# Causal mask of an attention layer: from matrix products to a select behind the exponential

## The chip, the cores and the metric

The kernel runs on one core of one Trainium2 chip. The metric is the device time of one execution in microseconds. The kernel before was run three times: 1224.71, 1217.82 and 1220.97 us, median 1220.97. One further execution was recorded by the hardware profiler; all rows and timelines here come from it. TensorE does the matrix products, VectorE (DVE) the maxima, ScalarE (ACT) the exponentials and most copies, GpSimd (POOL) some elementwise work and some transfers; SyncE (SP) issues most transfers.

## What is computed

The program is two transformer-like layers on x of shape (2, 1024, 256). Each adds an attention and a feed-forward branch of the normalised x to x. The change is in the attention of layer 0 only, which is causal: 32 query heads of 8 columns share 8 key and value heads.

```python
q = q * cos + rotate_half(q) * sin
k = k * cos + rotate_half(k) * sin
k_rep = jnp.repeat(k, KV_REPEAT, axis=1)
v_rep = jnp.repeat(v, KV_REPEAT, axis=1)
scores = jnp.einsum('bhqd,bhkd->bhqk', q, k_rep) / scale
scores = jnp.where((kpos > qpos)[None, None], -jnp.inf, scores)
attn = jax.nn.softmax(scores, axis=-1)
out = jnp.einsum('bhqk,bhkd->bhqd', attn, v_rep)
```

## The kernel before, in words

Queries are cut into blocks of 128: `(b, i)` is block i of batch b, and the order of the blocks is b = 0, i = 0 to 7, then b = 1, i = 7 to 0. A block attends to key blocks j = 0 to i; j = i is the diagonal, the only one with later keys in it.

**Scores are computed twice.** q and k are split into three bf16 parts each, stacked along the partitions: 64 rows of products (`qst[..][0]`, `kst[..][0]`) and 8 more (`[1]`). Two key heads (e = 0, 1) lie in partitions 0 to 63 and 64 to 127, so that each step issues two matmuls, one for each half of TensorE's rows.

- First, `max_unit` (L832) has queries as rows: it takes one to four heads and up to 512 keys in two PSUM buffers (pool `ps_s`, 3 buffers), and VectorE reduces them to a maximum for each query and head (L855). Only the largest 64 products go into it. On the block of keys with the diagonal the mask is added by matrix products with a half identity `ident_h` (L824): `mask_q`, in bf16, holds -1e30 where the key is later than the query and 0 elsewhere. The contraction runs over 64 rows, so that 128 queries take two products (t = 0, 1) for each half e, four in all. Where the block is 128 keys wide (i = 0 and 4), four heads are masked at once, with the mask broadcast to 512 columns; else each head's last 128 columns are masked in turn.
- Then the maxima are split, turned and written into three further rows of the query tile (`take_max`, `turn_max`), by way of HBM. So the second product gives scores less their maximum.
- `weigh` (L902) has keys as rows: for one key block j and one pair of key heads it makes two PSUM tiles of 128 keys x 512 (four heads x 128 queries; pool `ps_t`, 4 buffers) with products of 64 and of 35 rows (L907). On the diagonal four products with `mask_k` (L824, 512 columns each) add -1e30 for later keys. ScalarE takes the exponential into SBUF tiles `p` (L919, 7 buffers).
- `gather` (L925) multiplies the values, with a column of ones for the sum, by four such tiles (L927), and gathers over j in one PSUM bank, `acc`. After j = i the result is copied, turned, divided by the sum (`normalise`, L939), projected (`output`, L963) and added to x by GpSimd (L970).

**Order.** TensorE's instructions run in the order in which the program is written out (`manual_schedule`); the other engines' are ordered by a scheduler that follows priorities and its own estimate of when an operand is ready. Each engine then works strictly through its own list. The program is written in slots (`one_slot`, L1095). A slot issues as many maxima as a credit allows (the cost of a unit is 2 x heads x width), one piece of the feed-forward branch or of a weight conversion, and whatever an earlier slot put off by `after`; two slots go with each key block, one for each pair of heads. The loop at its end is this:

```python
one_slot(True)
if u and waiting:
    gather(*waiting)
group += weigh(b, i, 2 * G + u, j)
```

So a `gather` stands in TensorE's order two slots and one `weigh` behind the second `weigh` whose tiles it reads. Maxima run some ten slots ahead of their block and are used up about sixteen key blocks' slots before the end.

**GpSimd's other work in this stage:** four operations for each of 16 pieces of the feed-forward output (`out_piece`, L254 to L257), four for each of 12 ternary weight pieces behind VectorE's L332 and L333 (L334 to L337), rotations and splits of later queries and keys (L707, L709, L734), 16 additions to x (L970), a memset of later keys (L745), and transfers that load weights. At the very start it builds `ident_h`, `mask_q` and `mask_k` (L80, L84), ahead of the first weight loads of its queue (L216).

Behind layer 0, from about 800 us on, layer 1 runs; nothing of it is touched.

Of the kernel before, what the change touches and what calls it, by code (L numbers as in the profile page):

```python
# [15 lines left out]
ALU = mybir.AluOpType  # L16
# [3 lines left out]
P = 128  # L20
# [13 lines left out]
HALF = 64  # L34
AUG = 32
EXTRA = AUG + 3
NEG = -1e30
# [11 lines left out]
def two_layers(ctx: ExitStack, tc: tile.TileContext, a: dict, out: bass.AP):  # L49
    nc = tc.nc  # L50
# [22 lines left out]
    both = {}  # L73
    for name, op, fill, sign in (
        ("ident_h", ALU.not_equal, 1.0, 1),
        ("mask_q", ALU.is_ge, NEG, 1),
        ("mask_k", ALU.is_ge, NEG, -1),
    ):
        m = both[name] = zp.tile([P, 2, P], BF, tag=name, name=name)
        nc.gpsimd.memset(m, 0.0)  # L80
        for e in range(2):
            for t in range(2):
                part = m[HALF * e : HALF * e + HALF, t, :]
                nc.gpsimd.affine_select(  # L84
                    out=part,
                    in_=part,
                    compare_op=op,
                    fill=fill,
                    base=sign * HALF * t,
                    pattern=[[-sign, P]],  # L90
                    channel_multiplier=sign,
                )
    ident_h, mask_q, mask_k = both.values()
    groups = cp.tile([P, P], BF, tag="groups", name="groups")
    nc.vector.memset(groups, 0.0)
    nc.vector.memset(groups[0:64, 0:64], 1.0)
# [582 lines left out]
    def attention0(w, qlast, tables):  # L679
# [11 lines left out]
        with ExitStack() as es:  # L691
# [121 lines left out]
                for f in due:  # L813
                    f()

            def add_mask(out, mask, start, stop):

                for t in range(2):
                    for e in range(2):
                        rows = slice(HALF * e, HALF * e + HALF)  # L820
                        rhs = mask[rows, t, :]
                        if len(out[e].shape) == 3:
                            rhs = rhs[:, None, :].to_broadcast([HALF, 4, P])
                        nc.tensor.matmul(  # L824
                            out[e], ident_h[rows, t, :], rhs, start=start and t == 0, stop=stop and t == 1
                        )


# [3 lines left out]
            def max_unit(b, i, pairs, lo, width, part, masked):  # L832
                if (b, i) not in mx:
                    mx[b, i] = pool.tile([P, 2, 2, NH0 // 2], F32, tag="mx", name=f"mx{b}{i}", bufs=3)
                n = len(pairs)
                sc = [ps_s.tile([P, 512], F32, tag="s", name=f"m{b}{i}_{pairs[0]}_{part}{e}") for e in range(2)]
                four = masked and width == P
                if four:
                    add_mask([x.rearrange("p (h k) -> p h k", h=4) for x in sc], mask_q, True, False)
                for s, p in enumerate(pairs):  # L840
                    for e in range(2):
                        rows = slice(HALF * e, HALF * e + HALF)
                        nc.tensor.matmul(  # L843
                            sc[e][:, s * width : (s + 1) * width],
                            qst[b, i][0][rows, p, :],
                            kst[b][0][rows, p // 4, lo : lo + width],
                            start=not four,
                            stop=s == n - 1 if four else not masked,
                        )
                    if masked and not four:  # L850
                        end = (s + 1) * width
                        add_mask([x[:, end - P : end] for x in sc], mask_q, False, True)
                nonlocal reduced
                for e in range(2):
                    reduced = nc.vector.tensor_reduce(  # L855
                        mx[b, i][:, part, e, pairs[0] : pairs[0] + n],
                        sc[e][:, : n * width].rearrange("p (s k) -> p s k", s=n),
                        AX.X,
                        ALU.max,
                        negate=True,  # L860
                    )
# [27 lines left out]
            def max_units(b, i):  # L889

                if i > 3:
                    for p in range(16):
                        yield 1024, lambda p=p: max_unit(b, i, [p], 0, 512, 1, False)
                lo = 512 * (i // 4)
                width = (i % 4 + 1) * P
                n = (4, 2, 1, 1)[i % 4]
                for p in range(0, 16, n):
                    yield 2 * n * width, lambda p=p: max_unit(b, i, list(range(p, p + n)), lo, width, 0, True)
                yield 0, lambda: take_max(b, i)


            def weigh(b, i, u, j):  # L902
                sc = [ps_t.tile([P, 512], F32, tag="t", name=f"s{b}{i}_{2 * u + e}_{j}") for e in range(2)]
                for n, height in enumerate((HALF, EXTRA)):
                    for e in range(2):
                        rows = slice(HALF * e, HALF * e + height)
                        nc.tensor.matmul(  # L907
                            sc[e],
                            kst[b][n][rows, u, j * P : (j + 1) * P],
                            qst[b, i][n][rows, 4 * u : 4 * u + 4, :],  # L910
                            start=n == 0,
                            stop=n == 1 and j < i,
                        )
                if j == i:
                    add_mask([x.rearrange("p (h q) -> p h q", h=4) for x in sc], mask_k, False, True)
                ps = []
                for e in range(2):
                    p = pool.tile([P, 512], F32, tag="p", name=f"p{b}{i}_{2 * u + e}_{j}", bufs=7)
                    nc.scalar.activation(p, sc[e], AF.Exp, scale=scale)  # L919
                    ps.append(p)  # L920
                return ps

# [192 lines left out]
            for n, (b, i) in enumerate(order):  # L1115
                if n and n + 3 < len(order):
                    load_q(*order[n + 3])
                while n not in done_at or slot < done_at[n] + (LEAD if n > 2 else SHORT):
                    one_slot(False)
                for G in range(2):  # L1120
                    for j in range(i + 1):
                        for u in range(2):
# [4 lines that stand above are left out]
                        waiting = (b, i, G, j, group)  # L1127
                        group = []
# [116 lines left out]
```

## Time and profile before

| | |
|---|---|
| median of three runs | 1220.97 us |
| profiled execution | 1217.11 us, its span 1215.3 us |
| busy, of the span | PE 1044.4 us, DVE 738.2, ACT 572.8, POOL 265.4 |
| mean granted TensorE clock | 0.903 |
| 100 to 760 us | PE busy 578.87 us, DVE 540.57, ACT 390.83, POOL 140.39 |
| 760 to 800 us | PE busy 39.53 us, DVE 6.83, ACT 27.90, POOL 7.30 |

In a row of the profile, "L824 PE MATMUL s<-mask_k,ident_h x256" names the line of the kernel, the engine, the operation, the tile that is written and the tiles that are read, and the count. Buffer numbers are left out of names: `s` are the tiles of shifted scores, `m` those of maxima, `p` the exponentials, `acc` the gathered output. Matmuls are pipelined: the start-to-start distance of two rows tells what one costs in a stream, not its own duration. PEld are loads of the stationary operand. A wait "A <- B: total, times, longest" is idle time of A's engine that ended when B was done. The chain that ended last is followed back from the last instruction.

### The profile page before, as it was taken

The numbers are of one execution on the slowest core, as the hardware profiler recorded it, in microseconds if no ns is written. First come the engines' busy times: TensorE is split into PE (matmuls) and PEld (weight loads), VectorE is DVE, ScalarE is ACT, GpSimd is POOL, SyncE is SP. The second block draws the span as 40 slices with busy tenths as digits, with TensorE's granted clock in tenths as the row PEclk, the third lists the DMA queues.
The fourth block names the chain that finished last, engine by engine and source line by source line (L and its number), as shares of the span: only waits on it lengthen the run. The fifth ranks groups of instructions, "written<-read, shape, count | busy, mean of one in ns | idle before, by whom it ended". The sixth has DMA issues, their size and how long they took to land.

```text
span 1215.3 us, 19246 instructions
## 1 busy us (share of the span) xinstructions
PE 1044.4 (86%) x7467; PEld 501.8 (41%) x7484; DVE 738.2 (61%) x1416; ACT 572.8 (47%) x990; POOL 265.4 (22%) x277
## 2 busy tenths in 40 slices
PE   6464897896988989898989998989999999998884
PEld 3233332232332223232323333335676676675673
DVE  7576988886867898788895889253223223323220
ACT  1113353662645757575767775741424414414421
POOL 3021022104053010501014115234313212312100
PEclk9576897997898989997999999999999999999785
DMA  6721001103011010100010110038211421411202
GB/s 193 168 80 37 22 15 38 26 2 90 1 26 27 2 26 18 35 1 18 10 27 3 25 26 5 3 30 120 54 28 45 75 40 45 77 39 28 44 11 53
DMA packets 79012, 49.01 MB, mean 40 GB/s; under 512 B 31720, under 2 KB 73704, under 8 KB 78920
## 3 DMA queue, kind: packets, MB, share of 16 engines
q1 hardware_dynamic: 75960, 43.58, 16.7%
q0 software_dynamic: 2960, 4.20, 1.7%
q8 instruction: 59, 0.97, 0.3%
q14 instruction: 33, 0.27, 0.1%
HBM read 33.59 MB, written 15.73 MB: 41 GB/s over the span
## 4 chain that ended last, share of the span: by engine, by line
PE 57%; DVE 21%; DMA 7%; issue 4%; ACT 4%; POOL 3%; SPq 2%; ACTq 0%; POOLq 0%; DVEq 0%
DVE mx L855 12%; PE acc L927 9%; PE s L907 8%; PE f1gu L610 7%; PE f1o L641 5%; PE m L843 4%; PE sk L520 3%; PE sq L485 3%; PE gu L284 2%; PE m L824 2%; PE s L824 2%; PE ao L586 2%; ACT p L528 2%; DMA qkv<-all 2%; PE acc L535 1%
## 5 line engine op out<-in xcount | busy, mean ns | idle before, releaser
L855 DVE TENSOR_REDUCE mx<-m 128x1 f32<-128x512 f32 (+3 forms) x608 | 373.3, 656 | 114.5 <-PE m L843 66.9
L919 ACT ACTIVATE p<-s 128x512 f32<-128x512 f32 x576 | 307.5, 603 | 163.5 <-PE s L907 115.3
L927 PE MATMUL acc<-p,v 128*9 128x512 f32 x1152 | 165.5, 626 | 0.0
L843 PE MATMUL m<-k,qmain 64*128 64x512 bf16 (+3 forms) x384 | 94.7, 368 | 44.3 <-DVE mx L855 28.4
L610 PE MATMUL f1gu<-xnT,wgu 128*128 128x512 f32 x256 | 118.9, 609 | 0.0
L843 PE MATMUL m<-kmain,qmain 64*128 64x512 bf16 (+3 forms) x384 | 82.4, 335 | 19.9 <-DVE mx L855 18.1
L824 PEld LDWEIGHTS <-ident_h 64*128 64x128 bf16 x1088 | 60.4, 97 | 92.3 <-issue 53.6
L843 PEld LDWEIGHTS <-qmain 64*128 64x128 bf16 x768 | 50.1, 100 | 89.0 <-issue 63.3
L824 PE MATMUL m<-mask_q,ident_h 64*128 64x128 bf16 (+1 forms) x832 | 82.0, 239 | 3.8 <-DVE mx L855 2.8
L618 DVE TENSOR_TENSOR h<-f1gu,h 128x512 f32<-128x512 f32 x32 | 22.1, 692 | 100.4 <-PE f1gu L610 97.0
L907 PE MATMUL s<-qlast,k 35*128 35x512 bf16 x288 | 66.3, 405 | 14.5 <-DMA qlast<-mscr 14.5
L907 PE MATMUL s<-qmain,k 64*128 64x512 bf16 x288 | 68.8, 409 | 11.3 <-ACT ob L252 5.8
L970 POOL TENSOR_TENSOR x<-x,aos 128x256 f32<-128x256 f32 x16 | 12.7, 792 | 300.5 <-ACT aos L969 300.5
L622 POOL TENSOR_TENSOR sq<-h 128x512 f32<-128x512 f32 x28 | 29.1, 1039 | 189.7 <-DVE h L618 189.7
L907 PEld LDWEIGHTS <-k 64*128 64x128 bf16 (+1 forms) x576 | 22.2, 97 | 114.5 <-issue 106.7
L610 PEld LDWEIGHTS f1gu<-xnT,wgu 128*128 128x128 f32 x256 | 48.1, 197 | 49.4 <-issue 49.3
L907 PE MATMUL s<-qmain,kmain 64*128 64x512 bf16 x288 | 64.2, 391 | 4.2 <-ACT p L919 2.4
L493 DVE TENSOR_REDUCE m<-sq 128x16 f32<-128x2048 f32 x16 | 36.7, 2292 | 44.8 <-PE sq L485 43.2
L907 PE MATMUL s<-qlast,klast 35*128 35x512 bf16 x288 | 61.2, 387 | 0.0
L641 PE MATMUL f1o<-k,h 128*128 128x256 f32 x256 | 58.9, 387 | 0.0
L641 PEld LDWEIGHTS f1o<-k,h 128*128 128x128 f32 x256 | 49.1, 194 | 8.2 <-issue 1.3
L907 PEld LDWEIGHTS <-kmain 64*128 64x128 bf16 x288 | 15.0, 94 | 78.1 <-issue 73.9
(267 smaller groups left out, 1588.1 us busy)
## 6 DMA issues: line engine op xcount, KB each, us to landing
qmain<-qscr SPq DMA_DIRECT2D x64, 96.0 KB
qkv<-all SPq DMA_DIRECT2D x16, 384.0 KB
qscr<-ptq SPq DMA_DIRECT2D x32, 96.0 KB
x<-in_x SPq DMA_DIRECT2D x16, 128.0 KB
qmain<-qscr SPq DMA_DIRECT2D x32, 64.0 KB
qs<-qkv SPq DMA_DIRECT2D x16, 128.0 KB
ks<-qkv SPq DMA_DIRECT2D x16, 128.0 KB
vs<-qkv SPq DMA_DIRECT2D x16, 128.0 KB
```

The source lines that it names most:

```text
L485: nc.tensor.matmul(ps[:, s, r, :], columns(q, slice(S * s, S * s + HD + 8), 4 * b + r), columns(k, slice(S * s, S * s + HD + 8), 4 * b + r ...
L493: nc.vector.tensor_reduce(m, ps, AX.X, ALU.max, negate=True)
L520: nc.tensor.matmul(ps[:, s, r, :], columns(k, slice(S * s, S * s + HD + 9), 4 * b + r), columns(q, slice(S * s, S * s + HD + 9), 4 * b + r ...
L610: nc.tensor.matmul(ps[g], wgu[:, k, g * HID + hc * P : g * HID + (hc + 1) * P], xnT[n][:, k, :], start=(k == 0), stop=(k == 1),)
L622: nc.gpsimd.tensor_tensor(sq, h, h, ALU.mult)
L641: nc.tensor.matmul(po, hs[hc // 2][:, hc % 2, i * P : (i + 1) * P], wp[:, hc, :], start=(hc == 0), stop=(hc == NHC - 1),)
L824: nc.tensor.matmul(out[e], ident_h[rows, t, :], rhs, start=start and t == 0, stop=stop and t == 1)
L843: nc.tensor.matmul(sc[e][:, s * width : (s + 1) * width], qst[b, i][0][rows, p, :], kst[b][0][rows, p // 4, lo : lo + width], start=not fo ...
L855: reduced = nc.vector.tensor_reduce(mx[b, i][:, part, e, pairs[0] : pairs[0] + n], sc[e][:, : n * width].rearrange("p (s k) -> p s k", s=n ...
L907: nc.tensor.matmul(sc[e], kst[b][n][rows, u, j * P : (j + 1) * P], qst[b, i][n][rows, 4 * u : 4 * u + 4, :], start=n == 0, stop=n == 1 and ...
L919: nc.scalar.activation(p, sc[e], AF.Exp, scale=scale)
L927: nc.tensor.matmul(acc[32 * s : 32 * s + HD0 + 1, :], vst[b][:, j, 4 * G + s, :], ps[s], start=(j == 0), stop=(j == i),)
```

## The change

In `weigh`, the four products with `mask_k` on a diagonal are gone, the second score product ends the sum, and behind each of the two exponentials GpSimd writes zeros, in place, where the key (partition) is later than the query. `mask_k` is not built any more. In `add_mask`, the products of t = 1 take only the columns from 64 on, since the mask's rows 64 to 127 hold nothing but zeros before them. Nothing else is changed: the slots, their costs, the order of the products that are left, all buffers and all transfers stay.

```diff
-        ("mask_k", ALU.is_ge, NEG, -1),
...
-            def add_mask(out, mask, start, stop):
+            def add_mask(out, start, stop):
+
 
                 for t in range(2):
+                    lo = HALF * t
                     for e in range(2):
                         rows = slice(HALF * e, HALF * e + HALF)
-                        rhs = mask[rows, t, :]
-                        if len(out[e].shape) == 3:
-                            rhs = rhs[:, None, :].to_broadcast([HALF, 4, P])
+                        rhs = mask_q[rows, t, None, lo:]
                         nc.tensor.matmul(
-                            out[e], ident_h[rows, t, :], rhs, start=start and t == 0, stop=stop and t == 1
+                            out[e][:, :, lo:],
+                            ident_h[rows, t, :],
+                            rhs.to_broadcast([HALF, out[e].shape[1], P - lo]),
+                            start=start and t == 0,
+                            stop=stop and t == 1,
                         )
...
-                            stop=n == 1 and j < i,
+                            stop=n == 1,
                         )
-                if j == i:
-                    add_mask([x.rearrange("p (h q) -> p h q", h=4) for x in sc], mask_k, False, True)
                 ps = []
                 for e in range(2):
                     p = pool.tile([P, 512], F32, tag="p", name=f"p{b}{i}_{2 * u + e}_{j}", bufs=7)
                     nc.scalar.activation(p, sc[e], AF.Exp, scale=scale)
+                    if j == i:
+
+                        by_head = p.rearrange("p (h q) -> p h q", h=4)
+                        nc.gpsimd.affine_select(
+                            out=by_head,
+                            in_=by_head,
+                            compare_op=ALU.is_ge,
+                            fill=0.0,
+                            base=0,
+                            pattern=[[0, 4], [1, P]],
+                            channel_multiplier=-1,
+                        )
                     ps.append(p)
                 return ps
```

More of the change, by code (lines that the diff above doesn't have):

```diff
@@ L92, in two_layers @@
                 )
-    ident_h, mask_q, mask_k = both.values()
+    ident_h, mask_q = both.values()
     groups = cp.tile([P, P], BF, tag="groups", name="groups")
@@ L838, in max_unit @@
                 if four:
-                    add_mask([x.rearrange("p (h k) -> p h k", h=4) for x in sc], mask_q, True, False)
+                    add_mask([x.rearrange("p (h k) -> p h k", h=4) for x in sc], True, False)
                 for s, p in enumerate(pairs):
@@ L851, in max_unit @@
                         end = (s + 1) * width
-                        add_mask([x[:, end - P : end] for x in sc], mask_q, False, True)
+                        add_mask([x[:, None, end - P : end] for x in sc], False, True)
                 nonlocal reduced
```

## The prediction

> **What bounds the kernel now.** I read the slices first, then the chain that ended last by stage, then the waits.
>
> ```profile
> PE   6464897896988989898989998989999999998884
> DVE  7576988886867898788895889253223223323220
> POOL 3021022104053010501014115234313212312100
> ```
>
> Layer 0's attention fills slices 4 to 26, 100 to 800 us. TensorE is at 80 to 90%, VectorE close behind it, GpSimd mostly idle. Asked for 100 to 760 us and for 760 to 800 us, the chain that ended last gives:
>
> ```profile
> by line: DVE mx L855 21.8%; PE acc L927 14.7%; PE s L907 13.9%; PE m L843 6.5%; PE gu L284 4.4%; PE m L824 3.6%; PE s L824 2.9%; issue 2.4%; PE ot L942 1.7%; ACT p L919 1.4%; PE ao L966 1.3%; PE f0o L244 1.2%; DVE fs L291 1.0%; DVE xn L173
> ```
>
> ```profile
> by line: PE acc L927 35.2%; PE s L907 24.7%; PE s L824 13.0%; PE ot L942 7.4%; PE ao L966 5.3%; PE f0o L244 3.8%; ACT o L936 3.0%; PE lnt L178 2.6%; PE m L824 2.1%; ACT p L919 1.5%; PE m L843 1.2%; PE at L958 0.5%; issue 0.3%; PE mt L878 0.
> ```
>
> The chain changes between TensorE's matmuls and VectorE's maxima (L855); after 760 us, with the maxima done, it is TensorE alone. "PE s L824" is the mask in shifted scores (removed), "PE m L824" that in maxima (shortened). The waits, for 100 to 800 us, say how firm each engine's lead is:
>
> ```profile
> DVE mx L855 <- PE m L843: 59.6, 50, 5.5
> ...
> DVE mx L855 <- PE m L824: 45.8, 50, 7.2
> ...
> PE m L843 <- DVE mx L855: 42.0, 77, 1.9
> ```
>
> Where the maxima wait for TensorE they wait 1.05 us on average (105.4 us, 100 times); where TensorE waits for them, 0.55 us.
>
> **The change part by part.**
>
> ```profile
> L824 PE MATMUL m<-mask_q,ident_h x832: 213/216/631, 30.1 to 766.0; 64*128 64x128 bf16 x154, 64*128 64x512 bf16 x13
> L824 PE MATMUL s<-mask_k,ident_h x256: 373/376/631, 104.3 to 796.4; 64*128 64x512 bf16 x128
> ```
>
> 1. Mask products in shifted scores: 256 matmuls, four in each of 64 diagonal calls of `weigh`. The two halves run side by side: in the timeline pairs of 512 columns start 0.215 us apart, so a call loses 0.43 us, 27.5 us in all. On the chain they are 2.9% of 660 us, 19.1 us, up to 760 us (the last part is step 4). A saving of 0.43 to 0.86 us per diagonal passes a VectorE that waits 1.05 us, and stops at a shorter wait; I take three quarters, **-14.3 us** (bounds: a third and all, -6.4 and -19.1).
>
> 2. Fewer mask columns in maxima: of each four products, the pair of t = 1 shrinks. The 128-column pairs number 192; pairs start 0.055 us apart (525.741, 525.796 us), with their weight loads between. No row shows 64 columns; if loads set the spacing the gain is 0, if columns do, 0.027 us: 0 to 5.3 us. The 16 pairs of 512 columns become 256: 0.107 us each, 1.7 us. Half of the first plus the second, times three quarters: **-3 us** (bounds -1.3 and -5.3 at that share). The Trainium skill (TensorE: Matmul & The Clock Gate, "Back-to-back issue gap") gives columns / 2.4 + 2.5 ns for a full clock, with about 25 ns as floor; 128 columns then take 56 ns, which the trace's 55 ns agrees with, and by it 64 columns would take 29, nearly the whole 5.3 us.
>
> 3. 128 selects on GpSimd, 128x512 f32 in place, four for each of 32 diagonal gathers. The form is shown only small:
>
> ```profile
> L84 POOL TENSOR_SCALAR_AFFINE_SELECT mask_k<-mask_k x4: 285/288/293, 4.5 to 5.3; 64x128 bf16<-64x128 bf16 x4
> ```
>
> One of 128x128 f32 took 284 ns, a one-element memset 101 ns. With 101 ns fixed, the rest times four gives 0.83 us; with memset's slope (128 f32 205 ns, 576 f32 636 ns: 0.96 ns an element) 0.65 us. I take S = 0.72. Two-input products of 128x512 f32 at 1.04 to 1.27 us are a far upper row. The Trainium skill (GPSIMD Engine Reference, "3.1 Elementwise") has 512 elements of a one-input loop at 769 ns; with that, steps 3 and 4 would be 1.2 us longer.
>
> GpSimd's 128 x 0.72 = 92 us lie in its idle time (140.4 us busy of 660). What counts is when the gather's matmuls may start. The last two exponentials of a diagonal end 0.49 us apart; ACT to GpSimd takes 0.13 us, GpSimd to TensorE about 0.1 (short waits in the timeline). The fourth tile is then ready R = -0.49 + 0.13 + 2S + 0.09 = 1.17 us after its exponential's end, instead of 0.05. I read in the timeline how long after that end each diagonal gather starts. An example, b = 0, i = 7:
>
> ```profile
> 471.03 2.06 ACT L919 ACTIVATE p<-s 128x512 f32<-128x512 f32 x4 [0.49 <-PE s L824]
> ...
> 472.51 1.04 PE L927 MATMUL acc<-p,v 128*9 128x512 f32 x8
> ```
>
> The second of these four exponentials, the diagonal's last, ends at 472.11: margin 0.40 us, 0.77 short. Of the 27 diagonals before 770 us, 18 have margins of 1.17 us or more (up to 19.6); the others (1.15, 1.13, 1.07, 0.92, 0.81, 0.81, 0.78, 0.40, 0.35) fall short by 3.1 us together; three quarters is **+2.3 us**. With S = 0.60 it is 1.1, with 0.83 3.9.
>
> 4. The last five diagonals, with nothing between products and exponentials. In three TensorE already waits tile by tile:
>
> ```profile
> 776.48 1.89 PE L927 MATMUL acc<-p,v 128*9 128x512 f32 x8
> 776.85 0.10 PEld L927 LDWEIGHTS acc<-p,v 128*9 128x9 f32 x2 [0.27 <-ACT p L919]
> 777.34 0.10 PEld L927 LDWEIGHTS acc<-p,v 128*9 128x9 f32 x2 [0.39 <-ACT p L919]
> ```
>
> Four exponentials follow each other there, so only the first call's mask counts: 0.43 gained, 1.12 lost. The other two (margins 0.79 and 0.20) gain 0.86 and lose 0.38 and 0.97. Together 2.07 - 0.48 + 0.11: **+1.7 us**.
>
> 5. GpSimd's queue: a select starts behind what stands before it. `out_piece` puts 2.9 us there (L254 to L257); such a set ends 0.6 us after the last exponential of b = 1, i = 5, whose margin is 0.81, and one lies at b = 1, i = 2: some 1.3 and 0.7 us. In
>
> ```profile
> POOL tmg L334 <- DVE tlg L333: 125.5, 5, 34.7
> ...
> POOL klast L745 <- DVE fsw L196: 15.1, 1, 15.1
> ```
>
> the head of GpSimd's queue waits for VectorE. L745 runs at 113.65 for 1.81 us; if the first diagonal's selects (gather at 111.38) stand behind it, some 6 us go. I take half of that: **+5 us** with the sets (bounds 0 and 24, six diagonals at 4 us).
>
> 6. `mask_k` itself: 1.46 us of GpSimd at 3 to 6 us, ahead of weight loads whose data VectorE reads from 108 us; the chain there runs over SyncE's own loads. **0** (at most -1.5 if that cover goes). No transfer moves.
>
> Sum: -14.3 - 3 + 2.3 + 1.7 + 5 = **-8.3 us**. The profiled execution took 1217.11 us (span 1215.3, 1.8 around it), so 1208.8 there; the median of the three runs is 1220.97, 3.9 above, and I predict against it: **1212.7 us**.
>
> **The rivals.**
>
> - VectorE takes the lead: it is busy 540.6 of 660 us, and mx is the chain's largest share. If a third passes: -6.4 - 1.4 + 1.0 + 1.7 + 2 = -3: 1218. Against it: the 1.05 us waits.
> - All passes, S = 0.60 and a free queue: -19.1 - 4.3 + 1.5 + 0.5 = -21: 1200.
> - Slower: the queue. Selects stand behind instructions that wait for VectorE (twelve ternary pieces, each 4.7 us of GpSimd from L334 to L337), and TensorE, in order, waits at the gather. Without step 5 the sum is -13.3; it turns at 13.3 us, three to four diagonals at 4 us. Six give +10.7: 1232. For it: the waits above; against: margins of 8 to 20 us where several such pieces run.
> - Selects are slower than their small form. GpSimd's L970 shows stretching:
>
> ```profile
> L970 POOL TENSOR_TENSOR x<-x,aos x16: 714/725/1489, 142.2 to 805.0; 128x256 f32<-128x256 f32 x16
> ```
>
> Doubled to S = 1.45, R = 2.63: step 3 becomes 16.6 and step 4 9.0 us, sum +13: 1234. Against it: one of 16 was doubled. The Trainium skill (Perfetto Trace Analysis, "Optimizing Scalar/DVE Operations") says that GpSimd and VectorE share a read port, so that moving work between them might not help; here work moves from TensorE, but this rival is that rule's result.
>
> **How the numbers follow.** Forecast 0.48, VectorE leads 0.17, all passes 0.12, the queue 0.15, slow selects 0.08. The range takes in 1200 and the two slower cases' middle with the bounds of step 5: 1198 to 1234. About 0.5%, 6.1 us, is what a measurement of this kernel can tell from no change. Four fifths of the forecast's chance lies beyond it: faster 0.48 x 0.8 + 0.12 = 0.50; same 0.48 x 0.2 + 0.17 = 0.27; slower 0.23.
>
> **What would show it.** Right: selects of 0.65 to 0.83 us; "PEld acc <- POOL p" waits of some 10 us, mostly under 1.2 us each and late in the stage; no "PE s" mask rows; maxima's waits for TensorE shorter. Wrong: gathers waiting over 3 us for GpSimd, selects over 1.2 us, or mx growing on the chain by what L824 loses.

## The result, and the profile after

The changed kernel takes 1212.91 us (median of 20 runs, 1207.62 to 1215.4), the kernel before in the same sessions 1218.19 us (20 runs). The ratio is 0.9946, 95% interval 0.9932 to 0.996: **6.6 us faster** (4.9 to 8.3). The profiled execution took 1211.61 us, span 1209.9, mean granted clock 0.897.

The slices of the changed kernel, TensorE, VectorE and GpSimd:

```profile
PE   5464888896888989897989998988999999998884
DVE  6677988995877998789895889162223323322220
POOL 2023233314144021612125337553313213212100
```

GpSimd is busy 348.4 us instead of 265.4, TensorE 1026.2 instead of 1044.4. Lines have moved: the masks of maxima are L823, their products L846, the maxima L858, score products L910, the exponential L920, the select L924, the gather L940. Two rows, by source line (least, median and longest duration in ns, first and last start, forms):

```profile
L924 POOL TENSOR_SCALAR_AFFINE_SELECT p<-p x128: 631/637/1180, 105.8 to 790.3; 128x512 f32<-128x512 f32 x128
```

```profile
L823 PE MATMUL m<-mask_q,ident_h x832: 187/213/631, 32.0 to 758.6; 64*128 64x64 bf16 x81, 64*128 64x128 bf16 x73, 64*128 64x256 bf16 x7, 64*128 64x512 bf16 x6
```

A select takes 0.637 us at the median and 0.685 on average; 13 of the 128 take over 0.83 us. The chain that ended last, for 100 to 760 us and then for 760 to 800 us:

```profile
by line: DVE mx L858 25.4%; PE acc L940 12.7%; PE s L910 12.1%; PE m L846 6.5%; PE gu L283 4.8%; PE m L823 2.7%; issue 2.4%; PE f0o L243 1.6%; PE ot L955 1.3%; ACT p L920 1.2%; DVE fs L293 1.0%; DVE fw L300 1.0%; DVE fs L290 1.0%; DVE xn L1
```

```profile
by line: PE acc L940 32.1%; PE s L910 13.3%; PE ao L979 10.4%; ACT p L920 10.3%; POOL p L924 7.9%; PE ot L955 7.7%; ACT o L949 5.8%; DVE wgu L1163 5.7%; PE pqk L435 3.5%; issue 2.7%; ACT oT L973 1.0%; ACT aos L982 0.9%; PE at L971 0.8%; DVE
```

"PE s" mask rows are gone, maxima have a larger share, and at the end of the layer the selects stand on the chain themselves, with 7.9% of 40 us. The waits for 100 to 800 us:

```profile
DVE mx L858 <- PE m L846: 56.3, 47, 5.1
...
PE m L846 <- DVE mx L858: 48.4, 76, 2.8
...
DVE mx L858 <- PE m L823: 36.6, 42, 6.5
...
PEld acc L940 <- POOL p L924: 11.9, 20, 1.1
```

Maxima wait 92.9 us for TensorE instead of 105.4; TensorE waits 48.4 us for maxima instead of 42.0; and 20 gathers or parts of one wait for selects, none over 1.1 us. The timeline of the changed kernel at the diagonal that stood as the example of step 4 (there at 776.48):

```profile
768.59 0.11 PEld L940 LDWEIGHTS acc<-p,v 128*9 128x9 f32 x4 [0.43 <-POOL p L924]
768.59 2.70 PE L940 MATMUL acc<-p,v 128*9 128x512 f32 x8
768.98 1.23 POOL L924 TENSOR_SCALAR_AFFINE_SELECT p<-p 128x512 f32<-128x512 f32 x2 [0.59 <-ACT p L920]
769.67 0.10 PEld L940 LDWEIGHTS acc<-p,v 128*9 128x9 f32 x2 [0.97 <-POOL p L924]
770.25 0.10 PEld L940 LDWEIGHTS acc<-p,v 128*9 128x9 f32 x2 [0.49 <-POOL p L924]
```

The gather takes 2.70 us instead of 1.89. With its tiles ready it takes 1.045 us; what a diagonal gather takes beyond that I call *drawn out*. Summed over the 27 diagonals before 770 us and the last five, this is 4.4 and 2.9 us in the kernel before and 7.9 and 6.3 in the changed one.

**Where the time went, by stage.** The stages end where a gather starts: that of the first diagonal, of b = 1, i = 7 (first pairs), of b = 1, i = 2 (first pairs), and then the end of layer 0's last gather. So the second stage is, roughly, batch 0 and the fourth holds the last five diagonals. Times of the kernel before, and differences from it (us), each from one profile:

| kernel | to the first | batch 0 | b = 1, i = 7 to 3 | last part | layer 0 in all |
|---|---|---|---|---|---|
| before | 111.4 | 427.7 | 228.4 | 31.5 | 799.0 |
| after | -1.6 | -0.2 | -5.7 | +0.6 | -6.9 |
| e1 no selects | -3.4 | -9.1 | -6.5 | -3.1 | -22.2 |
| e2 full columns | -0.6 | +0.9 | -3.4 | +0.9 | -2.2 |
| e10 no selects, full columns | -1.9 | -7.6 | -5.7 | -3.1 | -18.4 |
| e11 no selects, two buffers for maxima | -1.1 | -10.0 | -6.3 | -3.1 | -20.5 |
| e3 before with selects | +0.4 | +2.2 | +1.5 | +3.1 | +7.2 |
| e4 before with short columns | +0.2 | +2.1 | -1.2 | 0.0 | +1.1 |
| e6 selects aside | -1.1 | -4.7 | -3.1 | -3.1 | -12.0 |
| e7 two selects | -1.8 | +6.3 | +10.2 | +10.6 | +25.3 |
| e5 late gathers | -0.9 | -1.3 | -2.7 | -2.8 | -7.6 |
| e8 late gathers, no selects | -0.2 | -10.6 | -5.0 | -2.5 | -18.3 |
| e9 late at the end | -3.6 | +2.5 | -5.9 | -2.8 | -9.8 |
| e12 products in batch 0 | 0.0 | +0.2 | -6.1 | -2.5 | -8.5 |

After and e9 have one program up to the last part, and differ by 2.0 us in the first stage and 2.7 the other way in the second (0.7 in sum): single stages are good to 2 or 3 us. In the changed kernel most of the gain, 5.7 of 6.9 us, lies in the third stage. Batch 0 gains nothing and the last part loses 0.6. The profiled execution of e4 was the longest of its twelve, so its row is not a typical one. Layer 1, which is untouched, took between 2 us less and 4.5 us more from profile to profile; verdicts below rest on the ratios.

### The profile page after: what moved, and what is told of

It is laid out like the page before. It is cut to its first block, busy times and chain, and to the rows that moved or that the text cites. A ratio compares the mean times of both kernels' runs of the same rounds, so it can differ in the third digit from the quotient of the medians.

```text
span 1209.9 us, 18918 instructions
## 1 busy us (share of the span) xinstructions
PE 1026.2 (85%) x7228; PEld 490.2 (41%) x7228; DVE 741.5 (61%) x1416; ACT 571.7 (47%) x990; POOL 348.4 (29%) x400
## 4 chain that ended last, share of the span: by engine, by line
PE 55%; DVE 26%; ACT 5%; issue 4%; POOL 4%; DMA 4%; SPq 1%; ACTq 0%; POOLq 0%; DVEq 0%
DVE mx L858 14%; PE f1gu L609 9%; PE acc L940 8%; PE s L910 7%; PE f1o L640 5%; PE m L846 4%; PE sk L519 3%; PE sq L484 3%; PE gu L283 3%; ACT p L527 2%; PE m L823 2%; PE acc L534 1%; PE ao L585 1%; PE pqk L435 1%; ACT p L920 1%
## 5 line engine op out<-in xcount | busy, mean ns | idle before, releaser
L858 DVE TENSOR_REDUCE mx<-m 128x1 f32<-128x512 f32 (+3 forms) x608 | 373.1, 654 | 101.5 <-PE m L846 63.1
L920 ACT ACTIVATE p<-s 128x512 f32<-128x512 f32 x576 | 307.1, 604 | 146.3 <-PE s L910 144.8
L940 PE MATMUL acc<-p,v 128*9 128x512 f32 x1152 | 173.7, 626 | 0.6 <-ACT o L949 0.2
L846 PE MATMUL m<-k,qmain 64*128 64x512 bf16 (+3 forms) x384 | 96.6, 376 | 49.2 <-DVE mx L858 33.0
L924 POOL TENSOR_SCALAR_AFFINE_SELECT p<-p 128x512 f32<-128x512 f32 x128 | 84.6, 685 | 170.1 <-ACT p L920 169.9
L846 PE MATMUL m<-kmain,qmain 64*128 64x512 bf16 (+3 forms) x384 | 82.8, 336 | 22.9 <-DVE mx L858 20.7
L846 PEld LDWEIGHTS <-qmain 64*128 64x128 bf16 x768 | 50.4, 101 | 88.4 <-issue 62.9
L910 PE MATMUL s<-qlast,k 35*128 35x512 bf16 x288 | 66.5, 411 | 14.6 <-DMA qlast<-mscr 14.6
L910 PE MATMUL s<-qmain,k 64*128 64x512 bf16 x288 | 68.6, 412 | 11.8 <-ACT ob L251 6.2
L823 PEld LDWEIGHTS <-ident_h 64*128 64x128 bf16 x832 | 44.9, 97 | 82.5 <-issue 60.3
L823 PE MATMUL m<-mask_q,ident_h 64*128 64x128 bf16 (+3 forms) x832 | 75.3, 222 | 2.5 <-DVE mx L858 2.2
L910 PE MATMUL s<-qmain,kmain 64*128 64x512 bf16 x288 | 64.0, 391 | 6.0 <-ACT p L920 3.2
L910 PEld LDWEIGHTS <-k 64*128 64x128 bf16 (+1 forms) x576 | 21.2, 97 | 115.7 <-issue 108.2
L910 PE MATMUL s<-qlast,klast 35*128 35x512 bf16 x288 | 61.3, 387 | 0.0
L983 POOL TENSOR_TENSOR x<-x,aos 128x256 f32<-128x256 f32 x16 | 13.1, 817 | 140.1 <-ACT aos L982 140.0
```

The costliest lines, as they stand in the source:

```text
L823: nc.tensor.matmul(out[e][:, :, lo:], ident_h[rows, t, :], rhs.to_broadcast([HALF, out[e].shape[1], P - lo]), start=start and t == 0, stop ...
L846: nc.tensor.matmul(sc[e][:, s * width : (s + 1) * width], qst[b, i][0][rows, p, :], kst[b][0][rows, p // 4, lo : lo + width], start=not fo ...
L858: reduced = nc.vector.tensor_reduce(mx[b, i][:, part, e, pairs[0] : pairs[0] + n], sc[e][:, : n * width].rearrange("p (s k) -> p s k", s=n ...
L910: nc.tensor.matmul(sc[e], kst[b][n][rows, u, j * P : (j + 1) * P], qst[b, i][n][rows, 4 * u : 4 * u + 4, :], start=n == 0, stop=n == 1,)
L924: nc.gpsimd.affine_select(out=by_head, in_=by_head, compare_op=ALU.is_ge, fill=0.0, base=0, pattern=[[0, 4], [1, P]], channel_multiplier=-1,)
L940: nc.tensor.matmul(acc[32 * s : 32 * s + HD0 + 1, :], vst[b][:, j, 4 * G + s, :], ps[s], start=(j == 0), stop=(j == i),)
```

## The experiments

My first theory was that of the prediction: the products' removal passes in full or nearly so, and the selects cost what the gathers wait for them (*the gate*), plus disturbances in GpSimd's queue. The rival was that **VectorE leads** in batch 0, so that taking work from TensorE gains nothing there. A second rival came up on the way: the selects lengthen VectorE's own instructions (*company*). Ratios are against the kernel before, with 95% intervals.

**e1, no selects.** Later keys within a diagonal block keep their weights, so part of the mask is left out.

```diff
-                    if j == i:
-
-                        by_head = p.rearrange("p (h q) -> p h q", h=4)
-                        nc.gpsimd.affine_select(
...
-                        )
```

> The changed kernel without the selects: later keys of a diagonal keep their weights, so that part of the mask is left out and the time shows the removal of the products and the shorter columns alone. By the steps of the prediction (products -14.3 before 770 us and -3.0 in the last five diagonals, columns -3.0, nothing for selects or queue): 20.3 us faster than before, ratio 0.983. If VectorE sets the pace until about 540 us and the saving arrives only behind it: the change's measured -6.6, less some 4.7 us that selects cost in the last five diagonals and 1 us before, so about 12 us faster, ratio 0.990, with at most 3 us of it gained before 540 us.

Measured: 0.9819 (0.9789 to 0.9849), 1195.29 us, 22 us faster. The products and columns gain what steps 1 and 2 and the 3.0 us of step 4 give together (20.3), and batch 0 gains 9 us. So VectorE does not lead in batch 0: without selects, TensorE's saving passes there too.

**e2, all mask columns in the maxima**, everything else as changed.

```diff
-                    lo = HALF * t
+                    lo = 0
```

> The changed kernel with all mask columns in the maxima, so only step 2 undone. By the steps of the prediction: 5.3 us faster than before (-8.3 + 3.0); against the changed kernel 3 us lost. If VectorE leads: the short columns are worth 1 us or less, some 5.5 to 6.5 us faster than before, ratio 0.995.

Measured: 0.9979 (0.9961 to 0.9997), 1214.62 us. The short columns are worth 0.0033 of 1218, 4.0 us (1.2 to 6.8).

**e3, the selects added to the kernel before**, whose products stay (so both mask).

```diff
                     nc.scalar.activation(p, sc[e], AF.Exp, scale=scale)
+                    if j == i:
+
+                        by_head = p.rearrange("p (h q) -> p h q", h=4)
+                        nc.gpsimd.affine_select(
...
+                        )
```

> The kernel before with the selects added behind the exponentials and the mask products kept, so that every select finds its zeros there already: the price of the selects alone. By the steps of the prediction: 2.3 us at the gathers before 770 us, 4.7 us at the last five, 5 us of queue: 12 us slower, ratio 1.010. If VectorE leads and the queue costs nothing: about 5 us slower, nearly all of it behind 770 us, ratio 1.004.

Measured: 1.0053 (1.0026 to 1.008), 6.5 us slower. That is half of what the step theory wanted, and less than half of the 15.5 us (0.9946 - 0.9819) that the same selects cost where the products are gone. In the table, nearly half of it is the last part (+3.1); batch 0 loses only 2.2. So the price of the same selects depends on what stands beside them. Two things differ and were not told apart: TensorE has more to do for each diagonal, and VectorE's own instructions are lengthened less (its busy time over the whole profile grows by 3.9 us, from 738.2 to 742.1).

**e4, short columns alone**, in the kernel before.

```diff
                 for t in range(2):
+                    lo = HALF * t if mask is mask_q else 0
...
-                            out[e], ident_h[rows, t, :], rhs, start=start and t == 0, stop=stop and t == 1
+                            out[e][:, :, lo:],
```

> The kernel before with the short mask columns in the maxima alone. By the steps of the prediction 3 us faster, ratio 0.9975 (bounds 1.3 to 5.3 us). If VectorE leads: 1 us or less, not told from no change.

Measured: 0.9989 (0.9967 to 1.0011), 1.3 us, not to be told from nothing; nor from e2's 4.0.

**e5, late gathers.** The gather of a diagonal is issued behind the score products that follow instead of ahead of them, to give its selects time.

```diff
-                            if u and waiting:
+                            late_one = waiting and waiting[3] == waiting[1]
+                            if u and waiting and not late_one:
                                 gather(*waiting)
                             group += weigh(b, i, 2 * G + u, j)
+                            if u and late_one:
+                                gather(*waiting)
```

> The changed kernel with the gather of a diagonal issued behind the weigh that follows it, not ahead of it: four products of 512 columns, 0.43 us, and what they wait for come first. If selects cost what TensorE waits for them at the gathers (gate theory): the diagonals' gathers are no longer drawn out (in the changed kernel by 14.2 us over 1.045 us each, without selects 7.7), 3 to 5 us faster than the changed kernel, ratio to before about 0.991. If they cost by their company on GpSimd, the shared port and the other engines' changed lists (company theory): within 1 us of the changed kernel, 0.995. The p tiles are held longer (7 buffers stay), which could take some of it back.

Measured: 0.9928 (0.9901 to 0.9955), some 2 us ahead of the changed kernel, not resolved. The last part gains 3.4 us against the changed kernel (drawn out 0.6 us instead of 6.3), the third stage loses 3.0. Before the last five diagonals the gathers are still drawn out by 6.5 us instead of 7.9, no more of a difference than between the changed kernel and e9 (7.9 and 9.5), which have one program up to there.

**e6, selects aside.** The selects read the same tiles at the same time but write to a tile of their own that nobody reads; weights of later keys stay. To make room, the maxima have two buffers instead of three.

```diff
+                        spill = pool.tile([P, 4, P], BF, tag="spill", name=f"spill{b}{i}_{2 * u + e}", bufs=1)
                         nc.gpsimd.affine_select(
-                            out=by_head,
+                            out=spill,
                             in_=by_head,
```

> The changed kernel with the selects reading p but writing a bf16 tile that nobody reads, so that gathers wait for the exponentials alone; later keys keep their weights, so that part of the mask is left out (and the maxima have 2 buffers in place of 3 to make room). Gate theory: as without selects, 21 to 22 us faster than before, ratio 0.982 to 0.984. Company theory: most of the selects' 15 us stays, ratio 0.990 or more.

Measured: 0.9875 (0.984 to 0.9909), 1205.2 us. The last part is that of the kernel without selects (-3.1), as the gate theory has it. But some 7 of the 15.5 us stay, though no gather waits for a select (one exponential does, once, for 1.3 us); in batch 0 4 to 5 us (-4.7 against -9.1 and -10.0).

**e7, each select twice.**

```diff
                         )
+                        nc.gpsimd.affine_select(
+                            out=by_head,
+                            in_=by_head,
...
+                        )
                     ps.append(p)
```

> The changed kernel with each select issued twice, so that its price is doubled (S from 0.685 to 1.37 us, R from 1.10 to 2.47): the rival of slow selects. Gate theory: by the margins read before, the shortfalls at the gathers before 770 us grow from 2.6 to 19.6 us, three quarters of that 13 us more, the last five diagonals 7 us more: 20 us slower than the changed kernel, ratio to before 1.011. Company theory: another 8 us or so, the gathers drawn out little more: ratio 1.001.

Measured: 1.0214 (1.0181 to 1.0248), 1244.23 us, 32.6 us behind the changed kernel, where 20 was expected. The waits for 100 to 830 us (L933 is the second select):

```profile
PEld acc L949 <- POOL p L933: 43.0, 50, 3.0
PE acc L949 <- POOL p L933: 9.9, 13, 2.1
```

Drawn-out gathers grow from 7.9 to 34.5 us before the last five and from 6.3 to 13.1 there: 33.4 us together, which is the whole loss. The expectation took GpSimd to be free for a diagonal's third tile as soon as its exponential ends. With 1.37 us for each tile and exponentials some 0.5 us apart it is not; that this makes up the missing 13 us was not tested by itself.

**e8, late gathers without selects**: the edits of e5 and e1 together; later keys keep their weights as in e1.

```diff
-                        nc.gpsimd.affine_select(
...
-                            if u and waiting:
+                            if u and waiting and not late_one:
```

> The late gather without selects, as a control of the order alone; later keys keep their weights, so that part of the mask is left out. Both theories: within 2 us of the kernel without selects, ratio to before 0.982 to 0.984; slower by more only if the p tiles, held longer, stop the exponentials.

Measured: 0.9859 (0.9824 to 0.9894). Behind e1 by some 5 us, not resolved (0.0040, half-width 0.0046). Of the 3.9 us between their two profiles in layer 0, some 3 lie ahead of the first diagonal's gather, and batch 0 is no slower. So a price of the late order is not shown. e9 uses it at the end only, the stage in which e5 gains.

**e9, late gathers in the last three blocks.**

```diff
+                            late_one = waiting and waiting[3] == waiting[1] and waiting[:2] in ((1, 2), (1, 1), (1, 0))
```

> The changed kernel, with the gather of a diagonal put behind the scores of the step that follows only in the last three query blocks (batch 1, blocks 2, 1, 0), as the run with late gathers had it everywhere. If the selects' price in the last five diagonals is the wait of TensorE at its gathers (6.3 us drawn out there in the changed kernel, 0.6 with late gathers), 3 to 5 us go and the middle stays as in the changed kernel: ratio to before about 0.9915. If the exponentials set the pace there, or the late order itself costs what it saves: within 1 us of the changed kernel, about 0.995.

Measured: 0.9925 (0.9896 to 0.9954), 1209.48 us. The last part gains 3.4 us against the changed kernel, as expected; by the ratios 2.6 us, not resolved. At the same diagonal as above, its timeline:

```profile
768.87 0.86 PE L910 MATMUL s<-qmain,kmain 64*128 64x512 bf16 x2 [0.30 <-ACT p L920]
...
769.88 1.31 PE L940 MATMUL acc<-p,v 128*9 128x512 f32 x8
```

Two score products run while the selects do, and the gather then takes 1.31 us instead of 2.70.

**e10, no selects and all mask columns**: only the mask products of the scores are gone (later keys keep their weights). Its edits are those of e1 and e2.

```diff
-                    lo = HALF * t
+                    lo = 0
...
-                        nc.gpsimd.affine_select(
```

> The changed kernel without the selects (later keys keep their weights within a diagonal chunk, that part of the mask is left out) and with all mask columns in the maxima, so that only the mask products in the shifted scores are gone against before. If these products are worth what steps 1 and 4 of the prediction gave (14.3 + 3.0 = 17.3 us): ratio 0.985 to 0.986, some 4 us behind the kernel without selects. If some 4.7 us of that kernel's lead were an early start of its own, at a higher granted clock ahead of 125 us, that does not come back here: about 0.989.

Measured: 0.9847 (0.9812 to 0.9881), 18.6 us (14.5 to 22.9). The products alone are worth about what the prediction gave them.

**e11, no selects, two buffers for the maxima** (weights as in e1): what e6 gave up.

```diff
-                    mx[b, i] = pool.tile([P, 2, 2, NH0 // 2], F32, tag="mx", name=f"mx{b}{i}", bufs=3)
+                    mx[b, i] = pool.tile([P, 2, 2, NH0 // 2], F32, tag="mx", name=f"mx{b}{i}", bufs=2)
```

> The changed kernel without the selects (later keys keep their weights within a diagonal chunk, that part of the mask is left out) and with two buffers for the maxima of a block instead of three, as the run with selects set aside had. If that run's remaining price (ratio 0.9875 against 0.9819 without selects, some 7 us, with nobody waiting for a select) is the company that selects keep to VectorE, the missing buffer costs nothing: 0.982 to 0.984. If the buffer made it: 0.987 to 0.988.

Measured: 0.9824 (0.9799 to 0.985). The buffer costs nothing that can be seen, so e6's 0.0051 above it, 6.2 us (1.0 to 11.4), belongs to selects for which no gather waits. A row of e11 and one of e6, by windows, over batch 0 (start:end, length, then busy time and count of PE, PEld, DVE, ACT and POOL, granted clock, DMA share, GB/s):

```profile
110.29:527.99 417.70, 358.52 (x2480) 121.49 (x2478) 347.05 (x647) 233.46 (x443) 87.74 (x89) 0.90 0.10 25
```

```profile
110.29:533.32 423.03, 360.66 (x2480) 121.73 (x2478) 352.91 (x647) 233.69 (x443) 131.31 (x154) 0.90 0.10 25
```

The same number of VectorE instructions, 647, is busy 5.9 us longer beside the selects, at the same clock, and the stage is 5.3 us longer. It reaches TensorE as a longer wait for the maxima, here for 100 to 800 us in e11 and then in e6:

```profile
PE m L846 <- DVE mx L858: 49.1, 82, 4.4
```

```profile
PE m L846 <- DVE mx L858: 53.5, 83, 4.4
```

**e12, products in batch 0, selects in batch 1**, with e9's late gathers; the whole mask is computed.

```diff
+                if j == i and b == 0:
+                    for t in range(2):
+                        for e in range(2):
+                            rows = slice(HALF * e, HALF * e + HALF)
+                            nc.tensor.matmul(
+                                sc[e].rearrange("p (h q) -> p h q", h=4),
+                                ident_h[rows, t, :],
+                                mask_k[rows, t, None, :].to_broadcast([HALF, 4, P]),
...
-                    if j == i:
+                    if j == i and b == 1:
```

> The run with late gathers in the last three blocks, but with the mask products kept for batch 0 and the selects only for batch 1. If, as the stages of the traces say, the products that go from batch 0 gain 7 to 8 us and the selects that come there lose as much (2 us by gathers, the rest by VectorE's instructions that get longer), batch 0 comes out even, and the time is that of the late gathers' run within 1.5 us: ratio about 0.992. If the selects of batch 0 cost only what the gathers wait for there (2 us), giving up the products' 7 us shows: about 0.996 to 0.997.

Measured: 0.9907 (0.9882 to 0.9932), 1205.57 us. Giving the products of batch 0 back costs nothing that can be seen, as the stages said: there, the selects take all, or nearly all, that the products' removal gains. This is the best kernel here that computes the whole mask, 0.0039 (half-width 0.0029) ahead of the changed one; that it is ahead of e9 is not resolved.

## What the selects cost, and where

Two prices. e6 takes the first away and leaves the second, e11 has neither:

- **The gate**, some 7 us by the gathers. The changed kernel is 8.6 us (4.2 to 13.1) behind e6. Drawn-out gathers add up to 14.2 us in the changed kernel and to 6.5 to 7.7 in the three without selects that keep its order (e1, e10, e11). The last five diagonals' part, 3.7 us on the clock (+0.6 against -3.1), goes with e6, where nothing waits, and all but 0.3 of it with e9.
- **Company**, some 6 us (1.0 to 11.4; e6 against e11), ahead of the last part. Over the whole profile VectorE's 1416 instructions are busy 733.4 to 736.1 us in the four kernels with neither selects nor mask products in the scores (e1, e8, e10, e11), 736.8 and 738.2 in the two with products alone (e4, before), 741.5 to 743.6 in the six with 128 selects (after, e2, e3, e5, e6, e9) and 751.2 with 256 (e7). It can be seen instruction by instruction. VectorE in the changed kernel at 737 us, then GpSimd in the same window, then VectorE at the same place in the kernel before:

```profile
736.83 0.68 DVE L195 TENSOR_TENSOR fs<-fw,fe 128x1024 bf16<-128x1024 bf16 x1
737.42 0.68 DVE L858 TENSOR_REDUCE mx<-m 128x2 f32<-128x512 f32 x1
738.03 1.11 DVE L198 TENSOR_TENSOR act<-fs,fe 128x1024 bf16<-128x1024 bf16 x1
```

```profile
736.94 1.66 POOL L924 TENSOR_SCALAR_AFFINE_SELECT p<-p 128x512 f32<-128x512 f32 x2 [3.36 <-ACT p L920]
```

```profile
743.06 0.68 DVE L196 TENSOR_TENSOR fs<-fw,fe 128x1024 bf16<-128x1024 bf16 x1
743.78 0.69 DVE L199 TENSOR_TENSOR act<-fs,fe 128x1024 bf16<-128x1024 bf16 x1
```

The addition L195 runs first and keeps its 0.68 us; two selects that start behind it take 1.66 us instead of 1.23. The next operation on two SBUF operands, the subtraction L198, starts while the second select still runs and takes 1.11 us instead of 0.69. The maximum between them, which reads PSUM, keeps its 0.68. Each of the two that start second is longer by 0.42 or 0.43 us, where the first still had 0.57 us to run. Over 95 to 825 us the maxima do not change at all, while a short conversion between SBUF tiles does; rows of the changed kernel, then of e1 (busy us, mean ns, idle before):

```profile
L858 DVE TENSOR_REDUCE mx<-m 128x1 f32<-128x512 f32 x384 | 245.5, 682 | 63.0 <-PE m L846 45.0 <-PE m L823 17.5
...
L873 DVE CAST mp<-mx 128x32 bf16<-128x32 f32 x14 | 4.0, 287 | 0.1
```

```profile
L858 DVE TENSOR_REDUCE mx<-m 128x1 f32<-128x512 f32 x384 | 245.4, 682 | 62.2 <-PE m L846 43.3 <-PE m L823 18.2
...
L873 DVE CAST mp<-mx 128x32 bf16<-128x32 f32 x14 | 3.0, 217 | 0.1
```

The Trainium skill (SBUF — State Buffer, "SBUF: two separate sides") says that GpSimd and VectorE share one pair of ports under an exclusive lock. It counts a GpSimd instruction, and one of VectorE that is in a two-port mode or has two SBUF inputs (the latter only against a GpSimd instruction that reads SBUF); whichever starts first holds the pair for its whole instruction, and the other waits. The rows at 737 us agree in both directions, and the maxima's 682 ns too.

The kernel before shows the same thing with GpSimd's other work, and so it could have been read ahead of the change. Of VectorE's 96 elementwise operations on two 128x1024 bf16 tiles, the 13 that started while a GpSimd instruction ran took 1.03 us on average, the other 83 took 0.68 and none of them over 0.70. In the changed kernel it is 19 at 1.02 us and 77 at 0.68.

Gate and company make up 13 to 14 of the 15.5 us (11.4 to 19.5); the intervals leave the rest open. What also stays open: over batch 0 the granted clock was 0.88 to 0.89 in four of the five kernels whose in-place selects stand there without products (after, e2, e5, e9) and 0.90 to 0.91 in eight of the nine others, e6 among them (e4, without selects, had 0.89). By an estimate, two per cent of TensorE's 366 us would be 7 us, so this may hold part of what the changed kernel loses there against e6 (4.5 us). Against it speaks the fifth of those kernels, e7, which has each select twice and 0.91. Whether the clock is a cause was not settled.

## Why the prediction came out

The time was right: 1212.7 us predicted, 1212.91 measured. That it agrees to 0.2 us is luck. The difference to before was predicted as -8.3 us and is -6.6 by the ratio (-5.3 between the medians); the median of 20 runs of before, 1218.19, lies 2.8 us under that of the three runs which the prediction started from, and these two deviations nearly cancel. Inside the sum, savings and the selects' price were both a little larger than predicted, and one term stood for a cost that did not come. The terms:

- **Steps 1 and 2, and step 4's 3.0 us of products:** 20.3 predicted, 22.0 (18.4 to 25.7) by e1, 21.4 by e11. Products alone 17.3 against 18.6 (14.5 to 22.9) by e10. So the share of three quarters fits within the intervals. Batch 0 gains 7.6 to 10.6 us in the four kernels without selects (e1, e8, e10, e11), so the saving passes there too, as the argument from the maxima's waits had it.
- **Step 2 by itself:** 3 predicted, 4.0 (1.2 to 6.8) by e2; e10 against e1 has 3.4, not resolved. The undecided half is settled: at the place which the prediction used, the 64-column pair takes 0.028 us to the next product and the 128-column pair took 0.055. Four mask products and the one behind them, before and after:

```profile
525.74 0.27 PE L824 MATMUL m<-mask_q,ident_h 64*128 64x128 bf16 x4
525.85 0.38 PE L907 MATMUL s<-qmain,kmain 64*128 64x512 bf16 x2
```

```profile
524.67 0.25 PE L823 MATMUL m<-mask_q,ident_h 64*128 64x128 bf16 x4
524.75 0.38 PE L910 MATMUL s<-qmain,kmain 64*128 64x512 bf16 x2
```

  The columns set it, not the loads. With the 1.7 us of the 512-column pairs this makes 7.0 us raw and 5.3 at three quarters, the prediction's own bound and inside e2's interval. For 64 columns the formula of the Trainium skill (TensorE: Matmul & The Clock Gate, "Back-to-back issue gap") gives 29 ns; the page states it for a single product, and the pairs in this trace agree with it.
- **Step 3:** S = 0.72 against 0.685 measured. Drawn-out gathers before 770 us are 2.9 to 4.1 us longer than in the kernels without selects (3.1 raw predicted). The size is right, with some luck: from an exponential's end to a waiting select it took 0.067 us at the median, and from a select's end to the gather 0.052, where the prediction had 0.13 and 0.09. With these R is 1.00 us, and the same margins then give 1.9 us raw; what makes up the rest is open.
- **Step 4:** the selects' 4.7 measured 3.7, the products' 3.0 measured 3.1, the net +1.7 measured +0.6. Right in kind: the last part is the one stage in which the change loses.
- **Step 5** is the step that failed. It priced GpSimd's queue at 5 us. The memset of later keys (L745 before, L744 after) did come between selects (113.19 to 114.99 us, between selects that start at 112.61 and 114.94), but no gather waited over 1.1 us for a select anywhere. In its place stands a cost of about the same size, 6.2 us (1.0 to 11.4), that the sum did not have: VectorE's own instructions beside the selects. It stood in the text only as a rival, and in the wrong form: that rival had GpSimd's selects doubled. Only 13 of 128 were stretched past 0.83 us; the side that lengthens on the path is VectorE's.
- **Step 6** had 0. The ten kernels that do not build `mask_k` start the first diagonal's gather 0.2 to 3.6 us earlier than before, the three others that build it 0.0 to 0.4 us later. All ten also lack the mask products of the scores ahead of that gather, so the two were not told apart.

The selects in all were priced at 12.0 (2.3 + 4.7 + 5) and cost 15.5 (11.4 to 19.5). The rivals: VectorE in the lead (1218) falls with e1 and e10, yet its picture, no gain in batch 0, is what comes out *once the selects are there*: e3 loses 2.2 us there while the products stay, and by e12 the selects cost batch 0's whole gain when the products are gone. All passes (1200) is where the kernels without selects are (1195 to 1201). Slower by the queue: not seen. Slower by slow selects: e7 shows its price, +32.6 us at twice the length.

One of the signs was badly chosen. Maxima's share of the chain growing by what L824 loses was to mean that I am wrong. It grew, from 21.8 to 25.4%, by 3.6 points where L824 lost 3.8. But e10, which has the products' gain in full, shows it as well:

```profile
by line: DVE mx L858 25.1%; PE acc L928 13.9%; PE s L910 12.7%; PE m L846 6.2%; PE gu L283 4.4%; PE m L823 3.3%; issue 2.4%; PE ot L943 1.5%; PE f0o L243 1.4%; PE ao L967 1.3%; ACT p L920 1.3%; DVE fs L290 1.0%; DVE fs L195 0.9%; DVE xn L17
```

Where two engines alternate on the chain, taking work from one raises the other's share, whether the time falls or not. Stage lengths tell the two apart, shares do not.

## What to carry to other kernels

Work moved to an idle GpSimd has two prices: what waits for its result, and what its running does to VectorE's instructions on SBUF. The second shows in no wait for GpSimd, only in VectorE's durations and in who waits for VectorE; to see it, compare the durations of the same VectorE instructions, and run the new work once with its result read by nobody. Savings and costs do not add where two engines are nearly tied: the same selects cost 6.5 us beside the mask products and 15.5 without them (difference 9.0, half-width 5.2), so price each part in the kernel as it will be, and by stage, since a change that pays in one stage can be left out of another (e12).

## What the runs showed of the hardware

- An instruction of GpSimd and one of VectorE on SBUF tiles held each other up: 0.69 to 1.11 us for a subtraction of two bf16 tiles, 1.66 instead of 1.23 us for a pair of selects, with reductions out of PSUM untouched at 682 ns. In the changed kernel the longest case met a memset of 1.80 us: a 128x256 f32 operation of VectorE on one tile, 0.41 us at the median, took 1.74.
- A 128x512 f32 select in place took 0.637 us at the median, in bf16 out of f32 0.634: the output's type made no difference.
- Side by side on the two halves of TensorE's rows, a pair of mask products of 64 columns took 0.028 us to the next product where one followed at once, half of the 0.055 us at 128 columns, with the weight loads between.
- From the end of an exponential on ScalarE to the start of a GpSimd instruction that waited for it: 0.067 us at the median of 43; from a select's end to TensorE's weight load that waited: 0.052 us at the median of 26.
